# A graph layer and a routed expert layer on one core: two gather pitches in the planner, halved histogram digits, five lists of nodes, and a short write behind each long counting step

## The chip, the cores and the metric

The kernel runs on one core of a Trainium2 chip, as one launch. The metric is the device time of that launch in microseconds (us); the time shown for a kernel is the median of several runs, and one further execution is recorded by the hardware profiler.

The engines that occur below: TensorE (PE in the profile, PEld its weight loads) for matrix products, VectorE (DVE) and ScalarE (ACT) for elementwise work, GpSimd (POOL), which here mostly issues indirect DMAs (gathers and scatters by a list of row numbers), and SyncE (SP), which issues plain DMAs. Each engine runs its own instructions in program order and waits on semaphores for the others.

## The reference

`x` holds 128 graphs of 128 nodes with 256 features, 16384 nodes in all.

```python
# layer 0: graph layer, then a mixture of experts
x = x + gnn(layernorm(x), adj)        # relu((x + adj @ x) W1 + b1) W2 + b2, per graph
x = x + ffn(layernorm(x), edge_index)

# ffn
h = (x @ W_gat).reshape(M, HEADS, NUM_EXPERTS)            # 4 heads x 4 experts
src, dst = edges + self loops                             # 1048576 random edges
e = leaky_relu(a_src[src] + a_dst[dst], 0.2)
ee = exp(e - segment_max(e, dst)[dst])
alpha = ee / segment_sum(ee, dst)[dst]
agg = segment_sum(h[src] * alpha[:, :, None], dst) + b_gat
scores = layernorm(agg).reshape(M, HEADS, NUM_EXPERTS).mean(1)
topk_s, topk_i = top_k(scores, 2)
w = softmax(topk_s)
for ei in range(NUM_EXPERTS):
    g = where(topk_i == ei, w, 0).sum(-1)
    out = out + g * (gelu(x @ W1[ei] + b1[ei]) @ W2[ei] + b2[ei])
```

The numbers in `edge_index` run over 65536, four times the nodes, so about three targets in four lie outside and drop out of the sums. Which two experts a node takes depends on the attention over all of its edges, so an expert can be chosen only once the edges are sorted, gathered and summed.

## The kernel before

**Stage 1** (0 to about 690 us) computes the graph layer graph by graph and writes `x1` and its layernorm to HBM, with a table of 24 numbers a node for the attention (`table`: h, a_src, a_dst). Beside it the edges are prepared for the attention.

**Stage 2** (690 us to the end) has four strands.

*Counting* (`count_edges`, VectorE). Every partition holds 8192 edge targets as int16 numbers. `Runs` sorts them in runs by a network of maximum and minimum steps, most of them 2048 numbers long (`build`, L529, `_pairs`, L502, `merge`, L546, which keeps the larger half), `push` (L653, L659) then moves the sorted targets into cells, and `histogram` (L699) counts them: in 8 sets of 512 cells, VectorE writes a low digit (L720, L724) and a high digit (15 comparisons `is_ge`, L730) as 0 and 1, and TensorE multiplies the two (L738, 64 products of 128x64 a set) into counts, which ScalarE copies out. There is one buffer for the high digits; before it is written again the products of the set before must have read it.

*Gathering* (`Gathers.task`, GpSimd). The attention runs over blocks of 47 columns of edges; each column of the first 12 blocks is one indirect DMA of 128 rows (L866), 564 in all. Only a few blocks' buffers exist, so that block k+3 is begun when block k has been used. `ask` puts other indirect DMAs into the same queue: one "last row", 128 `fin` rows (states of finished nodes), 94 `r_x` gathers (rows of nodes for routed units) and 94 `out_dram` writes (L873). `wait` adds small copies (`seen`, L857).

*Attention* (`attend`, VectorE). Each block takes a dozen steps on VectorE (L1069 to L1130). For a 13th block `last_block` gathers the rows that it lacks as one more DMA (`e<-table,e`), spreads them by L1022 on VectorE and three products on TensorE (L1031). Blocks from the fifth on wait until the counts are there. As soon as enough blocks are done, `finish_attention` and `gates` choose the two experts for a range of graphs (`PARTS`, `PIECES`).

*Experts* (TensorE). The graphs 88 to 127 run all four experts on every node (dense units: 16 products at L1537, gelu on ScalarE at L1541, 32 products at L1556). They need no gate at first and fill TensorE while edges are counted. The nodes of graphs 0 to 87 are put into units of 256 that take the same pair of experts (routed units, 47 of them). `Routes.task` makes the lists of nodes for each stretch of graphs (`REACH`, four stretches ending at 32, 64, 82 and 88; the counts of units in them, `LISTED`, are 11, 16, 9 and 11): prefix sums, then for batches of 8 graphs a product of two 0/1 digits (L1464 makes `low`) into one table, from which node numbers and places come, and a DMA on SP that puts the nodes' weights beside their rows (`xr<-weight`). A routed unit gathers its rows (`r_x<-xr,nodes`), turns them by four transposes on TensorE (L1683) and one copy on ScalarE (L1687), runs 32 products at L1702 and 32 at L1556, is weighted on VectorE (L1725, L1735) and written out by GpSimd.

**What sets the order.** In stage 2 the order of instructions on every engine is fixed at build time by a planner (`Plan`): each strand is a Python generator, which issues its instructions, then yields what it thinks they cost (`yield 0.3 * (HHI - 1)`) or a condition (`plan.was("counts")`). `Plan.run` keeps a clock for each of GpSimd, TensorE and VectorE, and lets the engine that is furthest behind take its next task. A gather is put down at `GATHER_US` = 1.4. So a constant that no instruction uses can still move instructions past each other. The names that the following touches: `GATHER_US`, `PART` (gathers in one go), `PARTS`, `PIECES`, `REACH`, `BATCH`, `LOWS` (buffers of `low`), `Runs` and its loops, `push`, `histogram`, `Gathers.task`.

Of the kernel before, what the change touches and what calls it, by code (L numbers as in the profile page):

```python
# [25 lines left out]
P = 128  # L26
# [3 lines left out]
M = NB * P  # L30
# [6 lines left out]
EC = NE // P  # L37
# [16 lines left out]
CKC = 32  # L54
HSET = 512
HK = 8
HLO = 8
HHI = P // HLO
# [6 lines left out]
SECOND_US = 7.5  # L65
BARE_US = 6.95
TURN_US = 0.8
GATHER_US = 1.4
LAND_US = 4.0
AHEAD_US = 6.0  # L70
SCALAR_US = 4.0
# [5 lines left out]
AHEAD = (3, 4, 8)  # L77
AHEAD_BUFS = 2
HIST_US = 2.0
SLACK_US = 20.0  # L80
PART = 6
YIELD_US = 16.0
XBUFS = 7

PARTS = [
    (15, 0, 2), (24, 0, 3), (32, 0, 4), (43, 0, 5), (53, 2, 6), (64, 3, 7),
    (72, 3, 8), (82, 4, 9), (88, 4, 10), (106, 5, 11), (117, 7, 12), (128, 7, 13),
]  # L90
PARTS = [
# [1 line left out]
    for start, (stop, a, b) in zip([0] + [g for g, _, _ in PARTS], PARTS)  # L93
]
PIECES = [slice(a, b) for a, b in zip(
    (0, 32, 64, 82, 88, 106), (32, 64, 82, 88, 106, 128)
)]
MOST = 32
EARLY = 4


REACH = (32, 64, 82, 88)
NL = REACH[-1]
PAIRS = [(a, b) for a in range(X) for b in range(a + 1, X)]
SLOTS = 2 * P
# [9 lines left out]
BAD = 13  # L115
SPREAD = 10
SHIFT = 4
BATCH = 8
LOWS = 2
LIST_US = 0.05  # L120


# [10 lines left out]
class Pair:  # L133


    def __init__(self, a, b):
        self.cur, self.other = a, b
# [350 lines left out]
class Runs:  # L488

    def __init__(self, nc, a, b, length, n):
        self.nc, self.pair, self.length, self.n = nc, Pair(a, b), length, n

    def _pairs(self, d):

        nc, s = self.nc, self.n // self.length
        v = self.pair.cur[:, 0 : self.n].rearrange("p (k t d) -> p k t d", t=2, d=d * s)
        o = self.pair.other[:, 0 : self.n].rearrange("p (k t d) -> p k t d", t=2, d=d * s)
        for t, op in enumerate((ALU.max, ALU.min)):  # L500
            for cols, cost in self._cuts(self.n // 2, d * s):
                nc.vector.tensor_tensor(  # L502
                    o[:, :, t, cols], v[:, :, 0, cols], v[:, :, 1, cols], op=op
                )
                yield cost
        self.pair.swap()

    def _cuts(self, n, inner):
# [10 lines left out]
    def build(self):  # L519

        nc, n, s = self.nc, self.n, self.n // self.length
        run = 1
        while run < self.length:
            v = self.pair.cur[:, 0:n].rearrange("p (k t l s) -> p k t l s", t=2, l=run, s=s)
            o = self.pair.other[:, 0:n].rearrange("p (k t l s) -> p k t l s", t=2, l=run, s=s)
            a, b = v[:, :, 0, :, :], v[:, :, 1, ::-1, :]
            for t, op in enumerate((ALU.max, ALU.min)):
                for cols, cost in self._cuts(n // 2, s):
                    nc.vector.tensor_tensor(  # L529
                        o[:, :, t, :, cols], a[..., cols], b[..., cols], op=op  # L530
                    )
                    yield cost
            self.pair.swap()
            yield from self._clean(run // 2)
            run *= 2

    def merge(self, keep_all):

        nc, n, s = self.nc, self.n, self.n // self.length
        v = self.pair.cur[:, 0:n].rearrange("p (l t s) -> p l t s", t=2, s=s // 2)  # L540
        a, b = v[:, :, 0, :], v[:, ::-1, 1, :]
        out = self.pair.other
        for at, op in ((0, ALU.max), (n // 2, ALU.min))[0 : 2 if keep_all else 1]:
            half = out[:, at : at + n // 2].rearrange("p (l s) -> p l s", s=s // 2)
            for cols, cost in self._cuts(n // 2, s // 2):
                nc.vector.tensor_tensor(half[:, :, cols], a[:, :, cols], b[:, :, cols], op=op)  # L546
                yield cost
        if keep_all:
            d = self.length // 2
            self.pair.swap()  # L550

            self.length *= 2
            yield from self._clean(d)
        else:
            self.n //= 2
            self.pair.swap()
            yield from self._clean(self.length // 2)
# [13 lines left out]
def count_edges(tc, nc, c, sp, dram):  # L571

    raw = [c.counted_raw] + [sp.tile([P, 4096], I32, name=f"raw{i}") for i in range(2)]
    pick = picks(nc, sp)
    runs = Runs(nc, c.counted, raw[1].bitcast(I16), 32, EC)
    yield from runs.build()
    yield from runs.merge(False)
    yield from runs.to_one()
# [54 lines left out]
    low = dst.bitcast(F32)  # L633
# [17 lines left out]
    def push(value, moved, by, rate):  # L651
        for v in halves(w, 2 if rate == 1 else 1):
            nc.vector.tensor_single_scalar(  # L653
                moved[:, v], value[:, v], P * by, op=ALU.bitwise_xor
            )
            yield w / 1920 / 2 + 0.1
        for v in halves(w - by, 4 // rate):
            to = slice(v.start + by, v.stop + by)
            nc.vector.tensor_tensor(value[:, to], moved[:, v], value[:, to], op=ALU.min)  # L659
            yield (w - by) / 960 / 4 + 0.1  # L660

    by = CROW // 2
    while by >= P:
# [31 lines left out]
def by_group(t):  # L695
    return t.rearrange("p (g k) -> p g k", k=HK)


def histogram(nc, c, value, raw, pick, sp):  # L699


    plan = c.plan


    w = P * CKC
    n_sets, per = w // HSET, HSET // CKC
    low = sp.tile([P, HSET], I16, name="low_digit")
    high = raw[1].bitcast(BF16).rearrange("p (g h k) -> p g h k", h=HHI, k=HK)
    lows = raw[2].bitcast(BF16).rearrange(
        "p (b g l k) -> p b g l k", b=2, l=HLO, k=HK  # L710
    )
    nc.vector.memset(high[:, :, 0], 1.0)
    yield 0.6
    found = raw[0].bitcast(F16)
    cols = per * HLO * HK
    taken = plan.after(0.0)
    for s in range(n_sets - 1, -1, -1):
        cells = slice(s * HSET, (s + 1) * HSET)
        one = lows[:, s % 2]
        nc.vector.tensor_single_scalar(  # L720
            low, value[:, cells], 2 * M - 1 - (P - HLO), op=ALU.bitwise_and
        )
        for j in range(HLO):
            nc.vector.tensor_single_scalar(  # L724
                one[:, :, j], by_group(low), float(j), op=ALU.is_equal
            )
        yield 0.3 * (HLO + 1)
        yield taken
        for j in range(1, HHI):
            nc.vector.tensor_single_scalar(  # L730
                high[:, :, j], by_group(value[:, cells]), float(HLO * j), op=ALU.is_ge
            )
        yield 0.3 * (HHI - 1)
        yield plan.after(0.5)
        pt = c.ps_big.tile([P, G, D], F32, name="big").rearrange("p g d -> p (g d)")
        for b in range(per):
            for g in range(b * CKC // HK, (b + 1) * CKC // HK):
                nc.tensor.matmul(  # L738
                    pt[:, b * HLO * HK : (b + 1) * HLO * HK],
                    high[:, g].rearrange("p h k -> p (h k)"),  # L740
                    one[:, g].rearrange("p l k -> p (l k)"),
                    start=(g % (CKC // HK) == 0), stop=((g + 1) % (CKC // HK) == 0),
                )
        taken = plan.tensor(HIST_US, 1.0)
        nc.scalar.copy(found[:, s * cols : (s + 1) * cols], pt)
    yield taken
# [89 lines left out]
class Gathers:  # L836
# [50 lines left out]
    def block(self, k):  # L887

        pool = self.ahead if k in AHEAD else self.ga
        return pool.tile([P, CB, ROW], F32, name="hs")  # L890

    def ask(self, todo, name, how=None, soon=False):

        at = len(self.asked)
        if soon:
            at = sum(entry[3] for entry in self.asked)
        self.asked.insert(at, (todo, name, how or self.one, soon))

    def task(self):
# [6 lines left out]
        while True:  # L906
            self.wait()
            if self.asked:
# [6 lines left out]
                yield GATHER_US * len(now)  # L915
                if not rest:
                    plan.done(name, LAND_US)
            elif parts and self.room(parts[0][0]):
# [11 lines left out]
                for i in range(j.start, j.stop):  # L930
                    col = k * CB + i
                    self.one(self.rows[k][:, i, :], self.table, self.c.index[:, col : col + 1])
                yield GATHER_US * (j.stop - j.start)
                if j.stop == CB:
                    plan.done(f"block{k}", LAND_US)
            elif not parts and {"routed end", "ends end"} <= plan.at.keys():
# [1741 lines left out]
```

## Time and profile before

| what | us |
|---|---|
| runs | 2082.5, 2083.95, 2087.71 |
| median | 2083.95 |
| profiled execution | 2084.91 |
| its span (first to last instruction) | 2083.1 |
| TensorE busy in it | 1925.0 |
| VectorE busy | 1505.7 |
| GpSimd busy | 1103.7 |
| ScalarE busy | 846.5 |

The granted TensorE clock of that execution is 0.971 of full speed on the mean. The span in stretches, busy time of each engine:

| stretch (us) | PE | DVE | POOL | PEclk |
|---|---|---|---|---|
| 700 to 775 | 75.0 | 71.8 | 64.7 | 1.00 |
| 775 to 800 | 13.7 | 5.4 | 19.7 | 0.80 |
| 800 to 1000 | 200.0 | 196.2 | 164.4 | 1.00 |
| 1000 to 1025 | 25.0 | 2.1 | 19.1 | 1.00 |
| 1025 to 1140 | 95.7 | 89.6 | 93.2 | 0.91 |
| 1140 to 1321 | 181.0 | 76.1 | 141.2 | 1.00 |
| 1321 to 1425 | 102.8 | 81.8 | 81.8 | 1.00 |
| 1425 to 1460 | 24.1 | 3.6 | 20.4 | 0.80 |
| 1460 to 1850 | 369.3 | 239.0 | 293.3 | 1.00 |
| 1850 to 2084 | 207.9 | 157.4 | 100.9 | 0.96 |

How to read the lines that follow. A line of the waits names the engine, what it was about to write and its line, and after the arrow who released it: microseconds in total, how often, the longest. A line of the groups names line, engine, operation, output and input tiles with their shapes and the count; then busy time and the mean nanoseconds of one; then the idle time before them and what ended it. In a timeline, each line is a stretch of equal instructions: start, length, engine, line, and how many. [...]

### The profile page before, as it was taken

What the parts mean: (1) busy time and instruction counts of PE and PEld (TensorE: products, weight loads), DVE (VectorE), ACT (ScalarE), POOL (GpSimd) and SP (SyncE); (2) the same over time, 40 slices, a digit from 0 to 9 for tenths busy, and PEclk for the clock granted to TensorE, in tenths of its full rate; (3) what the DMA queues carried; (4) which work ended last, traced back from release to release, by engine and by line L of the source; (5) the groups of instructions that cost most, each with busy time, mean ns of one, the idle gap of its engine ahead of it and who ended that gap; (6) DMA issues with size and microseconds to landing.
All of it is one profiled execution on the core that took longest, in us unless ns stands there. A gap on an engine that the chain in (4) does not pass through costs nothing. (4 is left out here: it accounts for less than half of the span.)

```text
span 2083.1 us, 28131 instructions
## 1 busy us (share of the span) xinstructions
PE 1925.0 (92%) x8882; PEld 1443.8 (69%) x8882; DVE 1505.7 (72%) x3758; ACT 846.5 (41%) x1533; POOL 1103.7 (53%) x1064
## 2 busy tenths in 40 slices
PE   7999989889998897999969999997999999999996
PEld 4676667666666464666647666786888888788785
DVE  5989999849997887999585571473438768567586
ACT  5878544444453222333313333341333444344332
POOL 2110101110100888888887777776777777766431
PEclk9999989999998899999989999998999999999998
DMA  9988887696852211233131246325554466477865
GB/s 238 226 223 212 196 233 187 177 203 160 135 134 74 57 48 49 60 124 124 31 104 51 56 144 235 104 72 168 157 190 129 142 169 146 119 186 260 289 228 180
DMA packets 299122, 313.36 MB, mean 150 GB/s; under 512 B 111617, under 2 KB 239571, under 8 KB 298838
## 3 DMA queue, kind: packets, MB, share of 16 engines
q1 hardware_dynamic: 231350, 241.19, 36.6%
q0 software_dynamic: 67616, 70.28, 18.5%
q8 instruction: 75, 1.23, 0.2%
q14 instruction: 81, 0.66, 0.1%
HBM read 156.93 MB, written 130.32 MB: 138 GB/s over the span
## 5 line engine op out<-in xcount | busy, mean ns | idle before, releaser
L866 POOL DMA_INDIRECT hs<-table,index x564 | 643.6, 1141 | 166.7 <-issue 159.8
L1556 PE MATMUL big<-mw,m_hid 128*128 (+1 forms) x2784 | 628.3, 383 | 0.0
L1556 PEld LDWEIGHTS big<-mw,m_hid 128*128 128x128 f32 x2784 | 524.9, 191 | 85.8 <-issue 17.0
L1702 PE MATMUL m_phid<-m_xn,mw 128*128 128x256 f32 x1504 | 341.9, 385 | 31.1 <-ACT m_xn L1687 28.9
L1702 PEld LDWEIGHTS m_phid<-m_xn,mw 128*128 128x128 f32 x1504 | 285.6, 192 | 76.5 <-ACT m_xn L1687 34.6
L1563 ACT COPY m_out<-big 128x1024 f32<-128x1024 f32 x87 | 88.1, 1012 | 510.5 <-PE big L1556 504.7
L1537 PE MATMUL m_phid<-m_xn,mw 128*128 128x512 f32 x640 | 286.0, 598 | 10.2 <-issue 10.2
L1955 POOL DMA_DIRECT2D at<-in_adj_dram x31 | 41.9, 1353 | 433.7 <-DMA at<-self_eye 376.3
L2037 PE MATMUL big<-w_sb,hid 128*128 128x256 f32 x1024 | 238.9, 389 | 11.9 <-ACT h_t L2018 11.5
L2026 PE MATMUL p_hid<-h_t,w_sb 128*128 128x512 f32 x512 | 232.1, 603 | 10.5 <-ACT h_t L2018 7.2
L2037 PEld LDWEIGHTS big<-w_sb,hid 128*128 128x128 f32 x1024 | 195.5, 195 | 43.0 <-ACT h_t L2018 17.4
L1537 PEld LDWEIGHTS m_phid<-m_xn,mw 128*128 128x128 f32 x640 | 122.1, 192 | 144.9 <-issue 134.4
L1708 ACT ACTIVATE m_hid<-m_phid,r_b 128x256 f32<-128x256 f32 x376 | 155.7, 472 | 157.0 <-PE m_phid L1702 105.4
L2026 PEld LDWEIGHTS p_hid<-h_t,w_sb 128*128 128x128 f32 x512 | 94.7, 192 | 118.8 <-issue 97.9
L1541 ACT ACTIVATE m_hid<-m_phid,mb 128x512 f32<-128x512 f32 x160 | 109.1, 687 | 146.3 <-PE m_phid L1537 146.2
L866 POOL DMA_INDIRECT fin<-states,ends x128 | 137.8, 1077 | 37.6 <-issue 35.6
L1735 DVE SCALAR_TENSOR_TENSOR r_x<-m_out,r_x 128x256 f32<-128x256 f32 x188 | 87.0, 484 | 71.9 <-ACT m_out L1563 62.0
L866 POOL DMA_INDIRECT r_x<-xr,nodes x94 | 98.1, 1044 | 40.9 <-issue 26.5
L2030 ACT ACTIVATE hid<-p_hid,b_sb 128x512 f32<-128x512 f32 x128 | 87.1, 682 | 76.8 <-PE p_hid L2026 76.7
L873 POOL DMA_INDIRECT out_dram<-r_x,places x94 | 100.4, 1068 | 32.1 <-issue 14.7
L2009 POOL DMA_DIRECT2D xt<-b_sb x32 | 43.1, 1347 | 104.5 <-ACT xn L1893 57.3
L1725 DVE SCALAR_TENSOR_TENSOR r_x<-b_rows,r_x 128x256 f32<-128x256 f32 x188 | 86.8, 483 | 4.5 <-issue 1.1
(393 smaller groups left out, 2444.5 us busy)
## 6 DMA issues: line engine op xcount, KB each, us to landing
mw<-in_L_ffn_W_dram SPq DMA_DIRECT2D x102, 512.0 KB
states<-room SPq DMA_DIRECT2D x55, 564.0 KB
ys<-m_out SPq DMA_DIRECT2D x40, 512.0 KB
y_in<-ys SPq DMA_DIRECT2D x40, 512.0 KB
xt<-in_x_dram SPq DMA_DIRECT2D x32, 512.0 KB
xt<-b_sb POOLq DMA_DIRECT2D x32, 512.0 KB
x_d<-x SPq DMA_DIRECT2D x32, 512.0 KB
xn_d<-xn_t SPq DMA_DIRECT2D x32, 512.0 KB
```

Of the source, the lines that this page charges most:

```text
L866: self.nc.gpsimd.indirect_dma_start(out=out, out_offset=None, in_=rows, in_offset=bass.IndirectOffsetOnAxis(ap=index, axis=0),)
L873: sc = self.nc.gpsimd.indirect_dma_start(out=rows, out_offset=bass.IndirectOffsetOnAxis(ap=index, axis=0), in_=values, in_offset=None, bou ...
L1537: nc.tensor.matmul(p_hid, w1[:, k, f * P : (f + 1) * P], xn[:, k, :], start=(k == 0), stop=(k == 1),)
L1541: nc.scalar.activation(hid[:, f, :], p_hid, AF.Gelu, bias=b1[:, f : f + 1])
L1556: nc.tensor.matmul(p_y[:, s, :], hid[:, f, s * P : (s + 1) * P], w2[s // 2][:, f, :], start=(f == 0 and not b2), stop=(f == DH // P - 1 an ...
L1563: nc.scalar.copy(y, p_y)
L1702: nc.tensor.matmul(p_hid[:, half], w1[i][:, k, f * P : (f + 1) * P], xt[:, k, :], start=(k == 0), stop=(k == 1),)
L1708: nc.scalar.activation(hid[:, f, half], p_hid[:, half], AF.Gelu, bias=b1[i][:, f : f + 1])
L1735: self.nc.vector.scalar_tensor_tensor(x[:, s, D : 2 * D], y[:, 2 * i + s, :], x[:, s, 2 * D + i : 2 * D + i + 1], x[:, s, D : 2 * D], op0= ...
L2026: nc.tensor.matmul(p_hid, w1_sb[:, k, f * P : (f + 1) * P], h_t[:, k, :], start=(k == 0), stop=(k == 1),)
L2030: nc.scalar.activation(hid[:, f, :], p_hid, AF.Relu, bias=b1_sb[:, f : f + 1])
L2037: nc.tensor.matmul(p_y[:, s, :], hid[:, f, s * P : (s + 1) * P], w2_sb[:, f, :], start=(f == 0), stop=(f == DH // P - 1),)
```

## The change

It has five parts.

1. The planner puts a gather down at 1.42 us until the counts are there and at 1.33 afterwards (1.4 throughout before), and hands GpSimd three gathers at a time instead of six.
2. Behind each step of `Runs` and `push` whose planned cost is at least 1.0 us, VectorE writes 64 zeros a partition into a tile that nothing reads (`rest`). The program has 156 of these writes.
3. The high digits' buffer is cut in two halves. A set of 512 cells is compared in two halves of 256, each with its own wait for the products that read that half two halves earlier; the products of a set are issued in two halves.
4. The stretch of graphs 32 to 63 is listed in two parts, ending at 52 and at 64: five lists with 11, 10, 6, 9 and 11 units, 47 as before. `PIECES` and one entry of `PARTS` follow. 
5. Lists are made in batches of 6 graphs with three buffers, instead of 8 with two.

```diff
-GATHER_US = 1.4
+GATHER_US = 1.33
+BESIDE_US = 1.42
...
+REST = 64
+REST_US = 0.11
 SLACK_US = 20.0
-PART = 6
+PART = 3
...
-    (15, 0, 2), (24, 0, 3), (32, 0, 4), (43, 0, 5), (53, 2, 6), (64, 3, 7),
+    (15, 0, 2), (24, 0, 3), (32, 0, 4), (43, 0, 5), (52, 2, 6), (64, 3, 7),
...
-    (0, 32, 64, 82, 88, 106), (32, 64, 82, 88, 106, 128)
+    (0, 32, 52, 64, 82, 88, 106), (32, 52, 64, 82, 88, 106, 128)
...
-REACH = (32, 64, 82, 88)
+REACH = (32, 52, 64, 82, 88)
...
-BATCH = 8
-LOWS = 2
+BATCH = 6
+LOWS = 3
...
+    def rest(self, cost):
+
+        if cost < 1.0:
+            return cost
+        self.nc.vector.memset(self.pad, 0.0)
+        return cost + REST_US
...
                 nc.vector.tensor_tensor(
                     o[:, :, t, cols], v[:, :, 0, cols], v[:, :, 1, cols], op=op
                 )
-                yield cost
+                yield self.rest(cost)
...
+    pad = sp.tile([P, REST], F32, name="pad")
+    runs = Runs(nc, c.counted, raw[1].bitcast(I16), 32, EC, pad)
...
-            yield w / 1920 / 2 + 0.1
+            yield runs.rest(w / 1920 / 2 + 0.1)
...
-            yield (w - by) / 960 / 4 + 0.1
+            yield runs.rest((w - by) / 960 / 4 + 0.1)
...
-    taken = plan.after(0.0)
+    taken = [plan.after(0.0)] * 2
...
-        yield 0.3 * (HLO + 1)
-        yield taken
-        for j in range(1, HHI):
-            nc.vector.tensor_single_scalar(
-                high[:, :, j], by_group(value[:, cells]), float(HLO * j), op=ALU.is_ge
-            )
-        yield 0.3 * (HHI - 1)
-        yield plan.after(0.5)
+        yield 0.2 * (HLO + 1)
         pt = c.ps_big.tile([P, G, D], F32, name="big").rearrange("p g d -> p (g d)")
...
+        for half in range(2):
+            high = highs[:, half]
+            begin = s * HSET + half * HSET // 2
+            yield taken[-2]
+            for j in range(1, HHI):
+                nc.vector.tensor_single_scalar(
+                    high[:, :, j], by_group(value[:, begin : begin + HSET // 2]),
+                    float(HLO * j), op=ALU.is_ge,
+                )
+            yield 0.15 * (HHI - 1)
+            yield plan.after(0.5)
+            for b in range(half * per // 2, (half + 1) * per // 2):
+                for g in range(b * CKC // HK, (b + 1) * CKC // HK):
+                    nc.tensor.matmul(
...
+            taken.append(plan.tensor(HIST_US / 2, 1.0))
...
+    def pitch(self):
+        return GATHER_US if "counts" in self.plan.at else BESIDE_US
...
-                yield GATHER_US * (j.stop - j.start)
+                yield self.pitch() * (j.stop - j.start)
```

More of the change, by code (lines that the diff above doesn't have):

```diff
@@ L488, with __init__ @@
 class Runs:
-    def __init__(self, nc, a, b, length, n):
+    def __init__(self, nc, a, b, length, n, pad):
         self.nc, self.pair, self.length, self.n = nc, Pair(a, b), length, n
+        self.pad = pad
+    def rest(self, cost):
[3 more added lines that the diff above has]
+        return cost + REST_US
     def _pairs(self, d):
@@ L531, in build @@
                     )
-                    yield cost
+                    yield self.rest(cost)
             self.pair.swap()
@@ L546, in merge @@
                 nc.vector.tensor_tensor(half[:, :, cols], a[:, :, cols], b[:, :, cols], op=op)
-                yield cost
+                yield self.rest(cost)
         if keep_all:
@@ L574, in count_edges @@
     pick = picks(nc, sp)
-    runs = Runs(nc, c.counted, raw[1].bitcast(I16), 32, EC)
+    pad = sp.tile([P, REST], F32, name="pad")
+    runs = Runs(nc, c.counted, raw[1].bitcast(I16), 32, EC, pad)
     yield from runs.build()
@@ L707, in histogram @@
     low = sp.tile([P, HSET], I16, name="low_digit")
-    high = raw[1].bitcast(BF16).rearrange("p (g h k) -> p g h k", h=HHI, k=HK)
+    highs = raw[1].bitcast(BF16).rearrange(
+        "p (b g h k) -> p b g h k", b=2, h=HHI, k=HK
+    )
     lows = raw[2].bitcast(BF16).rearrange(
@@ L711, in histogram @@
     )
-    nc.vector.memset(high[:, :, 0], 1.0)
+    nc.vector.memset(highs[:, :, :, 0], 1.0)
     yield 0.6
@@ L715, in histogram @@
     cols = per * HLO * HK
-    taken = plan.after(0.0)
+    taken = [plan.after(0.0)] * 2
     for s in range(n_sets - 1, -1, -1):
-        cells = slice(s * HSET, (s + 1) * HSET)
         one = lows[:, s % 2]
         nc.vector.tensor_single_scalar(
-            low, value[:, cells], 2 * M - 1 - (P - HLO), op=ALU.bitwise_and
+            low, value[:, s * HSET : (s + 1) * HSET], 2 * M - 1 - (P - HLO),
+            op=ALU.bitwise_and,
         )
@@ L726, in histogram @@
             )
-        yield 0.3 * (HLO + 1)
-        yield taken
-        for j in range(1, HHI):
-            nc.vector.tensor_single_scalar(
-                high[:, :, j], by_group(value[:, cells]), float(HLO * j), op=ALU.is_ge
-            )
-        yield 0.3 * (HHI - 1)
-        yield plan.after(0.5)
-        pt = c.ps_big.tile([P, G, D], F32, name="big").rearrange("p g d -> p (g d)")
[L736 to L742, printed above, removed]
-                )
-        taken = plan.tensor(HIST_US, 1.0)
+        yield 0.2 * (HLO + 1)
+        pt = c.ps_big.tile([P, G, D], F32, name="big").rearrange("p g d -> p (g d)")
+        for half in range(2):
[6 more added lines that the diff above has]
+                    float(HLO * j), op=ALU.is_ge,
+                )
+            yield 0.15 * (HHI - 1)
[3 more added lines that the diff above has]
+                    nc.tensor.matmul(
+                        pt[:, b * HLO * HK : (b + 1) * HLO * HK],
+                        high[:, g % (HSET // 2 // HK)].rearrange("p h k -> p (h k)"),
+                        one[:, g].rearrange("p l k -> p (l k)"),
+                        start=(g % (CKC // HK) == 0), stop=((g + 1) % (CKC // HK) == 0),
+                    )
+            taken.append(plan.tensor(HIST_US / 2, 1.0))
         nc.scalar.copy(found[:, s * cols : (s + 1) * cols], pt)
-    yield taken
+    yield taken[-1]
     yield plan.after(2.0)
@@ L914, in task @@
                     self.asked.insert(0, (rest, name, how, soon))
-                yield GATHER_US * len(now)
+                yield self.pitch() * len(now)
                 if not rest:
```

## The prediction

> **What bounds the kernel now.** I read the busy shares first, then TensorE's waits behind stage 1, then those of VectorE and GpSimd, and last the timelines in which gathers meet counting.
>
> ```profile
> PE 1925.0 (92%) x8882; PEld 1443.8 (69%) x8882; DVE 1505.7 (72%) x3758; ACT 846.5 (41%) x1533; POOL 1103.7 (53%) x1064
> PE m_phid L1702 <- ACT m_xn L1687: 28.9, 24, 1.3
> PE big L738 <- DVE counted L730: 19.3, 1, 19.3
> PE pt L1031 <- DVE room L1022: 11.3, 1, 11.3
> PE m_phid L1537 <- issue: 10.2, 1, 10.2
> PE big L1683 <- DMA r_x<-xr,nodes: 10.0, 4, 4.7
> ```
>
> TensorE sets the time, and what can still be had is in these lines (total, times, longest, from 650 us on): one stall of 11.3 before the copied last row's products, one of 19.3 before the first histogram, 24 turns of 1.2, and 10.0 for rows of routed units. (The 10.2 of L1537 is before 690 and untouched.) The two long stalls go back to VectorE, and from there to gathers:
>
> ```profile
> DVE e L1083 <- DMA hs<-table,index: 23.1, 2, 22.8
> DVE room L1022 <- DMA e<-table,e: 21.8, 1, 21.8
> ```
>
> VectorE waits 21.8 for the one-row gather (GpSimd reaches it at 791.6), and 22.8 from 1000 to 1023 for block 3's last gather, the 204th, begun at 1020.4. So GpSimd's pace beside counting is behind both. Two timelines of 843 to 851 us (start, length) show that pace, first GpSimd, then VectorE:
>
> ```profile
> 845.52 0.95 POOL L866 DMA_INDIRECT hs<-table,index  x1 [0.30 <-issue]
> 846.78 1.96 POOL L866 DMA_INDIRECT hs<-table,index  x1 [0.30 <-issue]
> 849.05 0.95 POOL L866 DMA_INDIRECT hs<-table,index  x1 [0.30 <-issue]
> ```
> ```profile
> 845.56 2.36 DVE L502 TENSOR_TENSOR counted<-raw 128x2048 int16<-128x2048 int16 x2
> 847.96 2.36 DVE L502 TENSOR_TENSOR raw<-counted 128x2048 int16<-128x2048 int16 x2
> ```
>
> A gather that begins just ahead of a step takes 0.95 and the next follows 1.26 later; one that meets a running step takes 1.96, pitch 2.27. The extreme: seven gathers record as back to back for 7.86 us at 722 and the stretch moves at 2.5 each.
>
> **The change, part by part.** By the program order of before and after:
>
> *Rests.* 156 writes of 64 numbers join VectorE. The nearest rows:
>
> ```profile
> L1066 DVE MEMSET msg<- 128x20 f32 x1 | 0.1, 75 | 0.0
> L1050 DVE MEMSET pre<- 128x384 f32 x2 | 0.8, 378 | 0.1
> ```
>
> By interpolation 75 + 44/364 x 303 = 112 ns. A counting step is 1.14 start to start without a semaphore wait and 1.26 with one, mean 1.20; I take step plus rest as 1.25, which is +0.05 x 156 = 8 us. Ends: -6 if the rest lies wholly inside the wait that it displaces, +30 if each adds 0.11 and a second gap of 0.08. These 8 lie ahead of L1083 and the histogram, where VectorE has 22.8 of wait to pay with.
>
> What they buy is the gathers' pace. No row shows a gather beside such a write, so bounds: 1.26 if one always slips in, 2.27 if never. Between 700 and 1020 the pitch now is (1020.4 - 722.3)/181 = 1.65. I take 1.4: a stop each 1.25 us, nearly the gather's own 1.26, nearest the rows of 843 to 845. Then 181 x (1.65 - 1.4) = 45 us earlier at most; a later start and blocks' buffers eat part, so I put gather 204 at 984 instead of 1020, and the one-row gather at 773.
>
> [...]
>
> *The 11.3 at L1031.* With the row gathered 18 earlier and L1022 done by 779, TensorE, which arrives at 786, waits for nothing: -11.3, and -1.2 of slow clock behind it.
>
> *The 19.3 at L738.* VectorE reaches L1083 at about 980 (999 less the 21.8 it waited at L1022, plus rests), waits some 7 (0 to 22), and has the first half set ready at 1051 to 1062. The order puts one more dense unit (14.5) ahead of the histogram, so TensorE, which was there at 1057.5 (1076.81 less 19.34), comes at 1057.5 - 12.5 + 14.5 = 1059.5. Stall 0 to 3: -19 from the stall, and -1.6 since the first 64 products took 3.60 on a slowed clock against 2.03 later.
>
> *Halved digits.* 120 comparisons become 240. From 1073.41 on, 15 of them take 3.35, 0.223 each; the smallest operations of VectorE follow each other at 0.075 (the copies at 999.03, 999.10 and 999.17), so half the elements cost about 0.075 + 0.148/2 = 0.15: 240 x 0.15 - 120 x 0.223 = +9 us (ends 0 and +27). Per set VectorE then needs 9 x 0.23 + 30 x 0.15 = 6.6, beside TensorE's 7 us of expert products between two sets: hidden if just. 512 products stay 512.
>
> *Five lists.* Nodes of graphs 32 to 63 are listed in two goes. The order gains 52 list products (0.03 each), 52 operations of `low`, a further gates piece, four table loads of ScalarE (1.28 each, ScalarE is 41% busy): about +4 us with the half-set switches on TensorE, of which a wait for the second list's total, 0 to 2. VectorE's part lies beside routed units, where it is 239 of 390 us busy. The two pitches, the parts of three gathers and the batches of six issue nothing: they act through the order, which is counted here. In exchange, turns that stand directly ahead of their unit fall from 24 to 17: -7 x 1.2 = -8.5. There is also one more transfer of weights on SP's queue, for which GpSimd waits, with block gathers and later units' rows queued behind it:
>
> ```profile
> POOL r_x L866 <- DMA xr<-weight: 8.9, 1, 8.9
> ```
>
> Up to there the first routed unit's turn moves from 1321.8 to about 1292 (-11 -1 -19 -2 +4, rounded). TensorE alone would end its last product at 2007: before 2060, less 30, less 8.5, less about 16 us lost at units 7 and 8 (10.0 waiting, the rest clock).
>
> *GpSimd takes it back.* From block 3 on it works through a list of DMAs in fixed order:
>
> ```profile
> L866 POOL DMA_INDIRECT hs<-table,index x311 | 321.1, 1032 | 93.0 <-issue 87.3 <-DMA hs<-table,index 2.1 <-DMA r_x<-xr,nodes 0.9
> L866 POOL DMA_INDIRECT r_x<-xr,nodes x70 | 71.6, 1024 | 30.7 <-issue 19.4 <-DMA xr<-weight 8.9 <-PE m_phid L1702 1.5
> L866 POOL DMA_INDIRECT fin<-states,ends x74 | 71.6, 968 | 21.7 <-issue 20.4 <-DMA fin<-states,ends 0.6 <-ACT m_hid L1541 0.3
> L873 POOL DMA_INDIRECT out_dram<-r_x,places x60 | 62.5, 1042 | 19.1 <-issue 10.2 <-DVE r_x L1735 2.2 <-DVE low L1464 1.2
> ```
>
> In 1140 to 1850 that is 515 DMAs; less 10 of waits, 700/515 = 1.36 each. In the new order unit 31's rows are the 789th DMA from the first gather (now the 762nd). So they start at 984 + 585 x 1.36 + 9 for weights = 1789 and land 3.7 later, at 1793, while TensorE alone would be there at 1769: up to 24 us of new waits at L1683 between units 7 and 31. From unit 31 the order is TensorE's again: 238 to the last product (before 246, less its turns), and 23 from there to the end of the span. 1793 + 238 + 23 = 2054 for the span. The profiled execution was 1.8 over its span and 1.0 over the median, so the median comes at about 2054.5; I say 2054.
>
> **Rivals.** *Rests pay in full* (2041 to 2065): the above, gather 204 between 971 and 995.
>
> *No gather passes in a rest* (slower). The seven gathers that record as one block at 722, beside gaps of 0.04, speak for it; the quick passes ahead of a step speak against. GpSimd then stays at 1020, but the order asks unit 31's rows 27 DMAs later: 1020 + 585 x 1.36 + 9 + 4 = 1829, 15 behind today's 1814; with 238 + 23 and a few us of slow clock in those waits the time is 2095 (2090 to 2110). The dense unit drawn ahead fills a stall with work that is then missing later. It decides once gather 204 starts later than about 1013.
>
> *Half of it* (2065 to 2088): pitch near 1.5, gather 204 at 996 to 1012, or each of five weight transfers holding GpSimd 9 us at a bad moment.
>
> *GpSimd never binds* (2028 to 2041): its pitch falls to 1.30, as it is between 1075 and 1100 where few waits fall. 975 + 585 x 1.30 + 4 = 1740, ahead of TensorE's 1769, and 2007 + 23 = 2030 is left.
>
> **How the numbers follow.** Chances: full 0.52, half 0.22, none 0.16, never bound 0.10. The time is the first's; its own range is 2041 to 2065. The range 2036 to 2088 leaves out none passing and most of the last. A measurement tells 0.3% (6.3 us) from nothing: faster is below 2077.7, slower above 2090.2. Faster: 0.52 + 0.10 + 0.14 of the half case = 0.76; slower 0.16; same 0.08.
>
> **What would show it.** Right: gathers at 1.35 to 1.45 between 720 and 980; the waits at L1031 and L738 under 3; VectorE's wait at L1083 under 20; the first routed turn at 1285 to 1298; about 17 waits for m_xn; new waits of TensorE for `r_x`, 10 to 25 us in all. Wrong: gather 204 behind 1010 (rests don't pass); VectorE's counting steps over 1.30 with their rest (price); a histogram wait above 6 with gathers early (halved digits too dear); waits for `r_x` at nought, or above 40.

## The result, and the profile after

The changed kernel takes 2092.0 us in the median of 8 runs (2091.26 to 2097.43), the kernel before 2081.26 in 8 (2076.24 to 2087.71): ratio 1.0053, 95% interval 1.0035 to 1.0070. It is slower, by half a per cent. The forecast was 2054 and faster; the rival in which no gather passes in a rest said 2095. The profiled execution has a span of 2092.6 (2083.1 before).

Several chips took part, and on some of them TensorE's short products started 0.7 to 2.8 us apart from the histogram on and every kernel, the one before too, took 2310 to 2360, so that of those runs (e1 to e4, e13 to e16) only what lies ahead of the histogram is compared with the rest.

The busy shares and TensorE's waits from 650 us on, in the changed kernel (L1704 is L1683 of before, L1723 is L1702, L756 is L738, L1052 is L1031):

```profile
PE 1924.5 (92%) x8938; PEld 1442.9 (69%) x8938; DVE 1555.9 (74%) x4262; ACT 851.4 (41%) x1539; POOL 1107.6 (53%) x1064
```
```profile
PE big L1704 <- DMA r_x<-xr,nodes: 29.4, 6, 18.7
PE m_phid L1723 <- ACT m_xn L1708: 22.1, 16, 2.8
PE big L756 <- DVE counted L748: 12.2, 1, 12.2
PE m_phid L1558 <- issue: 10.1, 1, 10.1
PE m_phid L1723 <- DMA mw<-in_L_ffn_W_dram: 6.5, 1, 6.5
...
PE pt L1052 <- DVE room L1043: 2.6, 1, 2.6
```

TensorE is busy for the same 1925 us, so the loss is waits. Those ahead fell, if not all as far as meant: 11.3 to 2.6 at the last row, 19.3 to 12.2 at the histogram, 28.9 to 22.1 at the turns. The wait for rows of routed units rose from 10.0 to 29.4, and the one for expert weights from 2.0 to 6.5. VectorE's waits between 690 and 1140 are nearly what they were (23.1 and 21.8):

```profile
DVE e L1104 <- DMA hs<-table,index: 21.0, 1, 21.0
DVE room L1043 <- DMA e<-table,e: 20.4, 1, 20.4
```

So the gathers came hardly sooner. The timelines of GpSimd and of VectorE (start, length) show why; L503 is the new write:

```profile
721.72 1.99 POOL L884 DMA_INDIRECT hs<-table,index  x1 [0.30 <-issue]
724.01 2.00 POOL L884 DMA_INDIRECT hs<-table,index  x1 [0.30 <-issue]
726.32 2.00 POOL L884 DMA_INDIRECT hs<-table,index  x1 [0.30 <-issue]
728.63 0.95 POOL L884 DMA_INDIRECT hs<-table,index  x1 [0.31 <-issue]
```
```profile
721.70 0.11 DVE L503 MEMSET pad<- 128x64 f32 x1
721.73 1.16 DVE L513 TENSOR_TENSOR raw<-counted 128x2048 int16<-128x2048 int16 x1
...
724.00 0.11 DVE L503 MEMSET pad<- 128x64 f32 x1
724.03 1.16 DVE L540 TENSOR_TENSOR counted<-raw 128x2048 int16<-128x2048 int16 x1
...
728.61 0.11 DVE L503 MEMSET pad<- 128x64 f32 x1
728.68 1.23 DVE L513 TENSOR_TENSOR raw<-counted 128x2048 int16<-128x2048 int16 x1
```

At 721.70 and 724.00 the next step starts 0.03 us after the write does, the write still running by its record. Each of the first three gathers starts 0.01 to 0.02 after a write's start and is held for a whole step. It then ends so that its successor comes 2.29 to 2.31 later, which is two steps of 1.15: at the same point of the step, to be held again. At 728.61 the next step has a semaphore to wait for and starts 0.07 after the write, and the gather that comes between them passes. Of the gathers 23 to 204, these start between two operations of `Runs` of over 1 us each, by how long ahead of the next one:

| ahead of the step | before: passed, held | changed: passed, held |
|---|---|---|
| 0 to 25 ns | 3, 0 | 0, 19 |
| 26 to 100 ns | 31, 0 | 17, 0 |
| 101 to 500 ns | 2, 2 | 14, 0 |
| over 500 ns | 0, 27 | 0, 19 |

In the kernel before, a gather that comes in the last 100 ns ahead of the next step gets in, 34 of 34 (and in e1 and e11 below, without the write, all 9 that come in the last 25). With the write, it depends on what comes behind it. In the changed kernel the 19 gathers that start between a write and a long step of `Runs` 0.03 behind it are all held, the 15 ahead of a step that a semaphore keeps back to 0.07 all pass, and so do the 14 that start in the 0.15 us ahead of a write with no such semaphore behind it. Over the eight traces with writes of 64 (this one, e5, e9, e10, e13, e14, e16, e17) the three counts are 149 of 152 held, 128 of 128 passed and 108 of 108 passed. So in these traces a gather had to be there before the write started, as it had to be there before the step; beside the write it got in only where a semaphore kept the step back. Over all 181, 119 pass (records up to 1.2 us) and 61 are held (1.2 to 2.4; before 116 and 63); the pitch is 1.607 (1.647), and gather 204 starts at 1012.6 (1020.4; forecast 984).

One thing the writes do change. In the kernel before, a single gather is held through six steps that follow each other:

```profile
722.33 7.86 POOL L866 DMA_INDIRECT hs<-table,index  x1 [0.30 <-issue]
```
```profile
721.30 3.52 DVE L502 TENSOR_TENSOR raw<-counted 128x2048 int16<-128x2048 int16 x3
724.71 4.66 DVE L529 TENSOR_TENSOR counted<-raw 128x2048 int16<-128x2048 int16 x4
```

Each of the eight traces without writes (before, e1, e6, e7, e8, e11, e15, e18) has one such record of 7.9 to 9.0 us between 712 and 723; the eight with writes of 64 have none over 3.3. It is worth little: from the queue's first DMA to the 204th it is 327.5 us in the changed kernel, 332.9 and 332.7 in e1 and e11.

What follows is one order of DMAs on GpSimd. Unit 31's rows are the 789th, as forecast, and start at 1813.6, which is (1813.6 - 1012.6)/585 = 1.369 each. The dearest wait is at unit 7, here on TensorE and on GpSimd:

```profile
1430.02 0.44 PE L1704 MATMUL big<-ident,r_x 128*128 128x128 f32 x1 [18.66 <-DMA r_x<-xr,nodes]
```
```profile
1423.49 0.96 POOL L884 DMA_INDIRECT r_x<-xr,nodes  x1 [0.30 <-issue]
1424.75 0.96 POOL L884 DMA_INDIRECT r_x<-xr,nodes  x1 [0.30 <-issue]
```

From 1300 to these two no wait of GpSimd is over 0.3: it is simply not there yet. TensorE, whose first turn comes 10.4 earlier than before, gets to unit 7 ahead of rows that start only 2.9 earlier.

### The profile page after: what moved, and what is told of

The parts are those of the page before. It is cut to its first block, busy times and chain, and to the rows that moved or that the text cites. A ratio compares the mean times of both kernels' runs of the same rounds, so it can differ in the third digit from the quotient of the medians.

```text
span 2092.6 us, 28770 instructions
## 1 busy us (share of the span) xinstructions
PE 1924.5 (92%) x8938; PEld 1442.9 (69%) x8938; DVE 1555.9 (74%) x4262; ACT 851.4 (41%) x1539; POOL 1107.6 (53%) x1064
## 5 line engine op out<-in xcount | busy, mean ns | idle before, releaser
L884 POOL DMA_INDIRECT hs<-table,index x564 | 631.9, 1120 | 165.1 <-issue 155.8
L1723 PE MATMUL m_phid<-m_xn,mw 128*128 128x256 f32 x1504 | 340.9, 383 | 31.4 <-ACT m_xn L1708 22.1
L1723 PEld LDWEIGHTS m_phid<-m_xn,mw 128*128 128x128 f32 x1504 | 283.8, 191 | 73.1 <-ACT m_xn L1708 25.9
L1558 PE MATMUL m_phid<-m_xn,mw 128*128 128x512 f32 x640 | 287.6, 600 | 13.5 <-issue 10.1
L891 POOL DMA_INDIRECT out_dram<-r_x,places x94 | 106.0, 1127 | 31.5 <-issue 14.7
L884 POOL DMA_INDIRECT r_x<-xr,nodes x94 | 104.6, 1113 | 33.1 <-issue 25.1
```

Source lines behind the costliest of these rows:

```text
L884: self.nc.gpsimd.indirect_dma_start(out=out, out_offset=None, in_=rows, in_offset=bass.IndirectOffsetOnAxis(ap=index, axis=0),)
L891: sc = self.nc.gpsimd.indirect_dma_start(out=rows, out_offset=bass.IndirectOffsetOnAxis(ap=index, axis=0), in_=values, in_offset=None, bou ...
L1558: nc.tensor.matmul(p_hid, w1[:, k, f * P : (f + 1) * P], xn[:, k, :], start=(k == 0), stop=(k == 1),)
L1723: nc.tensor.matmul(p_hid[:, half], w1[i][:, k, f * P : (f + 1) * P], xt[:, k, :], start=(k == 0), stop=(k == 1),)
```

## The experiments: the writes

**e1, e11: the changed kernel's order without the writes.**

```diff
-        self.nc.vector.memset(self.pad, 0.0)
+        pass
```

> The changed kernel in its own order, without the 156 writes. Theory (the writes of 64 numbers, seen 0.03 us before the next step, are too short to let a gather in, and cost as little): gathers 23 to 204 keep a pitch of 1.60 to 1.66, gather 204 at 1010 to 1020, the time 2090 to 2098, ratio to before 1.004 to 1.009. Rival (the writes as built do let some in, and save the kernel from worse): pitch 1.75 or more, gather 204 behind 1030, 2103 to 2115.

> The kernel of e1 once more, with no writes in the changed kernel's order. Theory (the writes of 64 numbers move nothing): gather 204 at 1008 to 1020, ratio 1.002 to 1.008. Rival (they let gathers in): gather 204 behind 1025, ratio 1.010 or more.

Gather 204 at 1010.5 and 1016.9, pitch 1.586 and 1.585: without the writes the gathers from the 23rd on are no slower (1.607 with them; the long hold comes ahead of the 23rd in e1 and e11). e11's time is 2094.92, ratio 1.0041 (1.0025 to 1.0057), against 1.0053 with the writes: the intervals overlap. e1's time can't be compared. The writes are not what made the kernel slower, and gain nothing that the time shows. They cost next to nothing either: mean step 1.192 with and 1.178 without.

**e2, e3, e4, e12: writes of 128, 192 and 256 numbers, same order.**

```diff
-REST = 64
+REST = 256
```

> The changed kernel with writes of 128 numbers. Theory: a write of 128 is seen some 0.08 us before the next step, so step and write are 1.23; a gather that was held starts 0.13 ahead of a step and passes, and about one in four is held: pitch 1.45 to 1.55, gather 204 at 985 to 1000, the histogram's stall under 6, the time 2065 to 2082. Rival (a write of any length lets nothing in): pitch 1.60 or more, VectorE 8 us later per 156 writes, the time 2092 to 2102.

> The changed kernel with writes of 192 numbers. Theory: step and write are 1.28 or more, longer than a free gather's 1.26, so that nearly every gather passes: pitch 1.28 to 1.40, gather 204 at 965 to 985, stalls before the histogram and at the routed units 7 and 28 under 5 each, the time 2045 to 2070. Rival (a write of any length lets nothing in): pitch 1.60 or more, the histogram 10 to 20 us later than in the changed kernel, the time 2095 to 2115.

> The changed kernel with writes of 256 numbers. Theory: pitch 1.27 to 1.38 as with 192, but VectorE pays 0.19 to 0.2 for each write, some 8 us more in all than with 192, all ahead of the histogram: it is ready 0 to 8 later, the time 2045 to 2075, no better than with 192. Rival (a write of any length lets nothing in): pitch 1.60 or more, the time 2105 to 2125.

> The kernel of e4 once more, writes of 256 numbers in the changed kernel's order, where the chip before held TensorE back behind the histogram. Theory (writes this long let the gathers in, and those that are still held meet other operations): gather 204 at 992 to 1003, some 10 to 20 us ahead of the changed kernel, the histogram's stall under 9, waits for r_x of 10 to 20 us instead of 29, ratio 0.996 to 1.002. Rival (what GpSimd gains VectorE loses): ratio 1.004 or more.

The step is the mean from one step of `Runs` of 2048 numbers to the next where nothing but the write stands between them (99 pairs from 690 on).

| run | numbers | step | passed, held | pitch | gather 204 |
|---|---|---|---|---|---|
| e11 | none | 1.178 | 123, 57 | 1.585 | 1016.9 |
| changed | 64 | 1.192 | 119, 61 | 1.607 | 1012.6 |
| e2 | 128 | 1.236 | 133, 47 | 1.565 | 1005.9 |
| e3 | 192 | 1.290 | 143, 36 | 1.607 | 1014.5 |
| e4 | 256 | 1.357 | 143, 36 | 1.529 | 997.9 |
| e12 | 256 | 1.356 | 143, 35 | 1.569 | 1010.9 |

The same kernel's gather 204 differs by 6 to 13 us from chip to chip (e1 and e11; e4 and e12; 1009.3, 1016.1 and 1010.8 in e13, e16 and e17), so differences of that size in the last column say nothing.

Half of the theory stands: with longer writes more gathers get in. Of those between long steps of `Runs`, 66 pass at 101 to 300 ns ahead in e3, and 76 at 301 to 500 in e4; they start before the write does. In e2 the step follows 0.08 behind the write's start without a semaphore, and 4 of the 5 that start in between are held, so that it is hardly the distance that counts. But the pitches that I expected, 1.45 to 1.55 in e2 and 1.27 to 1.40 in e3 and e4, are missed, the latter by far, for three reasons that the traces show. Gathers that pass at each step go at the step's pace (the seven from 857.79 on in e4 start 1.34 to 1.36 apart), and the mean step is now 1.357 there. Of the 36 that are still held in e3 and in e4, 14 start between two long steps even so, and the rest meet other operations, of `attend` and of the counting. And in e3 GpSimd waits 19.6 us in seven `seen` copies, for marks that ScalarE sets. In e12 three gathers in a row are held for 10.5, 5.1 and 6.5 us from 716 on, in e4 none for over 2.9: most of what parts these two runs of one kernel lies there. e12's ratio is 1.0016 (0.9986 to 1.0047), so with 256 numbers the time can't be told from the kernel before, nor surely from the changed one.

## The experiments: the parts one at a time

**e6: the accounts and parts of three alone**, in the kernel before.

```diff
-GATHER_US = 1.4
+GATHER_US = 1.33
+BESIDE_US = 1.42
-PART = 6
+PART = 3
```

> The kernel before with the two pitches and parts of three alone. The order asks unit 31's rows as the 789th DMA, as the changed kernel does, instead of the 762nd. Theory (accounts): the stalls of 11 and 19 us stay, turns that stand directly ahead fall by five or six (7 us), and new waits for r_x of 15 to 35 us come, ratio 1.003 to 1.012. Rival (other parts of the change lose): ratio 0.994 to 1.001.

2099.95 beside 2081.55, ratio 1.0104 (1.0054 to 1.0153). TensorE's waits in it:

```profile
PE m_phid L1706 <- ACT m_xn L1691: 19.9, 17, 1.3
PE big L739 <- DVE counted L731: 18.2, 1, 18.2
PE big L1687 <- DMA r_x<-xr,nodes: 18.1, 9, 6.3
PE m_phid L1706 <- DMA mw<-in_L_ffn_W_dram: 12.4, 3, 6.6
```

Seven turns fewer stand ahead of their unit (9 us), the waits for rows grow by 8 and those for expert weights by 10, and 6.3 for a digit of the lists comes new: this part alone is slower, by constants that no instruction uses. Why the weights came late is not shown. Parts of three were not tried without the accounts; e10 and e17 below have them and are not slower than the kernel before.

**e7: the five lists alone. e8: the halved digits alone.** The diffs are parts 4 and 5, and part 3, of the change.

> The kernel before with five lists, pieces and batches of six alone; unit 31 stays the 762nd. Theory (accounts): nothing much, ratio 0.996 to 1.003. Rival (the fifth list costs): one more wait of GpSimd for weights of 9 us or a wait of TensorE for the second list's product, ratio 1.004 to 1.010.

> The kernel before with halved digits alone. Theory: 240 comparisons at 0.15 cost VectorE 9 us more than 120 at 0.223, spread over the sets and hidden beside TensorE but for the first, whose products begin after half of it, 1 us earlier: ratio 0.997 to 1.002. Rival (VectorE falls behind TensorE in the eight sets): waits at the histogram's products of 1 us and more in several sets, 5 to 15 us in all, ratio 1.003 to 1.008.

e7: 2084.75, ratio 1.0020 (1.0007 to 1.0033); e8: 2080.44, 0.9999 (0.9985 to 1.0014). Neither makes the loss; e7's 0.2% is the more of the two. In e8 TensorE waits 20.2 before the first set and not measurably in the others: the extra work of VectorE is hidden.

**e5, e9, e10: other accounts in the changed kernel**, the rest as it is.

```diff
-GATHER_US = 1.33
-BESIDE_US = 1.42
+GATHER_US = 1.37
+BESIDE_US = 1.6
```

(e9: 1.37 and 1.55; e10: 1.4 for both.)

> The changed kernel with the two pitches put down as its profile measures them: 1.6 beside counting, 1.37 afterwards. The order then asks the rows of routed unit 7 as the 451st DMA from the first gather instead of the 500th, those of unit 31 as the 723rd instead of the 789th. Theory (the accounts of 1.42 and 1.33 are below what GpSimd does, and the order made from them has TensorE wait for rows): waits for r_x fall from 29.4 us to under 8, and the time to 2058 to 2074, ratio to before 0.989 to 0.997. Rival (the loss comes from the five lists, the halved digits or the writes, whatever the accounts): the time stays at 2086 to 2098.

> The changed kernel with pitches of 1.55 beside counting and 1.37 afterwards. The order lies between the changed kernel's and e5's: unit 31's rows are the 759th DMA (789 and 723 there, 762 before), the last row of finished nodes the 843rd (835 and 871 there, 847 before). Theory (one GpSimd queue feeds two ends, TensorE's last unit and the sums of the dense units, and the accounts share it out): waits for r_x under 12 us, TensorE's last product at 2040 to 2058, the last sum within 15 us of it, the time 2060 to 2078, ratio 0.990 to 0.998. Rival (the rest of the change costs, too): 2079 or more.

> The changed kernel with the old single pitch of 1.4: unit 31's rows are the 750th DMA, the last row of finished nodes the 849th, 20 turns directly ahead of their unit. Theory (two ends): TensorE's last product at 2040 to 2058, the last sum at 2055 to 2070, the time 2064 to 2082, ratio 0.991 to 1.000. Rival (the rest of the change costs, too): 2083 or more.

e5, with the pitches that the profile itself shows, is as slow as e6: 2098.01, ratio 1.0084 (1.0066 to 1.0103). The waits for rows did fall, to 6.3, and TensorE ends at 2035.5, 40 us sooner than in the changed kernel. But the kernel doesn't end there. The last chain of waits of e5:

```profile
2068.81 8.60 DMA y_in<-ys
2077.46 0.04 issue
2077.50 0.50 DVE acc L2283
...
2086.28 2.19 DVE acc L2283 x6
```

The dense units' outputs are weighted and summed on VectorE (`acc`) when the gates of the graphs 88 to 127 are known, and these need the `fin` rows, which GpSimd fetches from the same queue. In e5 the last `fin` gather is the 871st and starts at 1991.6; in the changed kernel it is the 835th, at 1916.5. I hadn't seen this second end. e9's order turned out otherwise than its expectation says (unit 31's rows the 729th, the last `fin` the 861st): 2088.25, ratio 1.0008 (0.9995 to 1.0020). e10: 2086.77, ratio 1.0013 (0.9998 to 1.0027).

**e13 to e18: 1.36 and 1.35 behind the counts.**

```diff
-GATHER_US = 1.33
+GATHER_US = 1.36
```

> The changed kernel with pitches of 1.42 beside counting, as it has, and 1.36 afterwards instead of 1.33. Its order has 17 turns directly ahead, like the changed kernel's, unit 31's rows as the 759th DMA (789 there) and the last row of finished nodes as the 843rd (835 there). Theory (one GpSimd queue feeds two ends and what one gains the other loses; over seven runs on undisturbed chips TensorE's last product and the last sum add up to 4112 to 4133): both ends come at 2048 to 2066, sum 4105 to 4125, the time 2066 to 2082, ratio 0.992 to 0.999. Rival (the parts other than the accounts cost as much as they gain): ratio 1.001 or more.

> The changed kernel with 1.42 and 1.35: unit 31's rows as the 774th DMA, the last row of finished nodes as the 839th, 16 turns directly ahead. Theory (two ends): between the changed kernel and e13, TensorE's last product at 2056 to 2070, the last sum at 2040 to 2056, ratio 0.995 to 1.002. Rival (waits for r_x jump once the order is ahead of GpSimd at all): ratio 1.003 or more.

> The kernel of e13 in its own order without the 156 writes. Theory (writes of 64 numbers do nothing): within 0.3% of e13, gather 204 within 8 us of it. Rival (they are what makes e13 what it is): 0.4% or more slower than e13, gather 204 10 us later or more.

> The kernel of e13 once more (pitches of 1.42 and 1.36; unit 31's rows the 759th DMA, the last row of finished nodes the 843rd), since e13's chip issued TensorE's short products 0.7 to 2.6 us apart, the kernel before's too. Theory (two ends of one GpSimd queue): TensorE's last product and the last sum both at 2048 to 2066, the time 2066 to 2084, ratio 0.992 to 1.000. Rival (the parts other than the accounts cost as much as they gain): ratio 1.001 or more.

> The kernel of e13 a third time, in search of a chip on which the kernel before takes its 2081 to 2085. Theory (two ends of one GpSimd queue): TensorE's last product and the last sum both at 2048 to 2066, the time 2066 to 2084, ratio 0.992 to 1.000. Rival (the parts other than the accounts cost as much as they gain): ratio 1.001 or more. On a chip where the kernel before takes 2320 or more it tells nothing of either.

> The kernel of e17 without the 156 writes. Theory (writes of 64 numbers do nothing): ratio 0.989 to 0.996, gather 204 within 8 us of e17. Rival (they have a part in it): ratio 0.997 or more. On a chip where the kernel before takes 2320 or more it tells nothing of either.

e13 to e16 ran where TensorE's instructions came late (ratios 1.0020, 1.0018, 1.0067 and 1.0075, beside 2324 and 2330 for the kernel before) and settle nothing on the question; so e14's pitch of 1.35 stays open. e17, the same kernel as e13, has 2065.27 beside 2079.39: ratio 0.9925 (0.9901 to 0.9949). It is faster than both kernels. e18, without the writes, has 0.9919 (0.9900 to 0.9938): they have no part in it. The gain holds only where the kernel before takes about 2081: on the other chips this same kernel has 1.0020 (e13) and 1.0075 (e16). TensorE's waits in e17:

```profile
PE m_phid L1723 <- ACT m_xn L1708: 20.4, 17, 1.5
PE big L756 <- DVE counted L748: 13.1, 1, 13.1
PE big L1704 <- DMA r_x<-xr,nodes: 11.4, 4, 9.4
```

All but the last are nearly as in the changed kernel. The two ends side by side, from the traces (us; "routed" is from the first routed turn to TensorE's last product):

| kernel | unit 31's rows, last `fin` (DMA number) | first turn | TensorE's last product | routed | last sum |
|---|---|---|---|---|---|
| before | 762, 847 | 1321.8 | 2066.1 | 744.3 | 2067.2 |
| changed | 789, 835 | 1311.4 | 2075.5 | 764.1 | 2039.4 |
| e6 | 789, 837 | 1312.6 | 2079.7 | 767.1 | 2047.4 |
| e17 | 759, 843 | 1306.6 | 2048.9 | 742.3 | 2038.1 |
| e10 | 750, 849 | 1317.2 | 2058.9 | 741.7 | 2069.9 |
| e9 | 729, 861 | 1305.5 | 2041.4 | 735.9 | 2082.0 |
| e5 | 723, 871 | 1286.5 | 2035.5 | 749.0 | 2089.5 |

Rows of routed units late: TensorE's end is late. Rows late in favour of them: the last sum is. Against my theory the two do not simply add up: 4105 to 4125 was expected in e17 and its sum is 4087; the last sum, expected at 2048 to 2066, came at 2038.1. One reading of that, which no run tests, lies in GpSimd's longest pauses: in the changed kernel it stands 19.0 us before 1853.9 and 21.6 before 1969.0 in a `seen` copy, until ScalarE has set a mark; in e17 no pause between two of its DMAs from 1200 to 1990 is over 13.5. The first of the two lies ahead of the last `fin` gather (1916.5) and can have delayed the last sum; the second lies behind it and cannot. So where TensorE falls behind the order for want of rows, GpSimd may later be held by what TensorE hasn't done yet.

## Why the prediction was wrong

**The step that failed** is the gathers' pace under the writes: "I take 1.4: a stop each 1.25 us", and from it gather 204 at 984. Measured are a pitch of 1.607 and 1012.6, 28.6 us later: most of the 38.6 by which the span of 2054 was missed. Two things in it were wrong. The write's price: 0.112 us by its record, as interpolated, but only 0.03 of it before the next step starts, so that step and write are 1.15 to 1.22, not 1.25. And the idea that a write is a stop: a gather that starts beside one is held unless a semaphore keeps the next step back, and e1 and e11 show that the pitch is no slower without it. The ends that I gave, 1.26 and 2.27, held the measured one; what I chose between them was not the nearest row but a hope for a new one. The nearest was the pitch measured over the same stretch, 1.65. A reading was wrong, too: the record of 7.86 us at 722 is not seven gathers but one (x1), held through six steps, and so no evidence for the rival that no gather passes.

**A second step failed behind it**, the path to the end: "1793 + 238 + 23" lets unit 31's rows set the time. Their second gather starts at 1813.6, but TensorE turns them at 1827.3, 13.7 later and without a wait, where 3.7 to land was reckoned (1427.63 to 1431.33, the second of unit 7 in the kernel before). GpSimd's rows held TensorE earlier, at units 7 (18.7) and 28 (9.8), 29.4 in all where 10 to 25 was said.

**What rested on it.** The wait at L1104 was to shrink to some 7 and stayed at 21.0, so VectorE had the first half set ready at 1077 instead of 1051 to 1062, and TensorE, there at 1065 (forecast 1059.5), waited 12.2 and not 0 to 3. The first turn came at 1311.4, 19 later than the forecast 1292.

**What held.** The stall at the last row fell by 8.7, 5.0 of it since the rows came sooner (the row gather starts at 785.5, forecast 773, before 791.6) and 3.7 since TensorE comes half a dense pass later. Halved digits: 240 comparisons at 0.153 (0.15 said) for 120 at 0.222, 10 us on VectorE (9 said), hidden: in the rows of 1040 to 1150 VectorE is idle for 2.6 us ahead of the 240 operations, where it waited 24.5 ahead of the 120, and TensorE waits for them only ahead of the first set.

```profile
L748 DVE TENSOR_SCALAR counted<-raw 128x256 bf16<-128x256 int16 x240 | 38.1, 256 | 2.6 <-PE big L756 2.4
L503 DVE MEMSET pad<- 128x64 f32 x21 | 2.4, 112 | 0.0
```

The 156 writes, put at 8 us, cost about 2: 156 x 0.014, by the mean step of e11 and of the changed kernel (1.178 and 1.192). Most of a write's record of 0.112 lies under the next step, which starts 0.03 behind the write's start. Nor does a write let a gather in by itself: of the 19 that start between a write and a step 0.03 behind it, none passed.

Turns: 17 said, 16 seen. GpSimd from block 3 on: 585 DMAs at 1.36 and 9 for weights, 805 in all; measured 801. With 1012.6 put in for 984, the forecast's own sum gives 1012.6 + 805 + 3.7 + 238 + 23 = 2082 for the span, and the rival's, with some us of slow clock, 2095; the span was 2092.6. That the rival's number came so near is partly luck: it had gather 204 at 1020 and unit 31's rows landed at 1829, 7 and 12 us too late, and left out that TensorE would be behind these rows. The point that I gave for where the change turns into a loss, gather 204 behind 1013, is within a microsecond of where it came, but decides nothing: e18 has it at 1018.5 and is faster than the kernel before. What the rival had wrong is its order of causes: not the writes lose, the accounts do (e6, e17), since they ask for rows at a pace that GpSimd hasn't got: 1.33 behind the counts where 1.369 was measured, and with 1.36 the wait for rows fell from 29.4 to 11.4.

**What I had not looked at** is the second end. I followed TensorE to its last product and took the rest of the span as a tail of 23 us. (By the records that product ends at 2066.1 and not at 2060, and the tail is 17; the sum is the same.) In the kernel before the last sum came at 2067.2, one microsecond after TensorE's last product; that both ends fall together there was in its trace, and a DMA moved forward for one may then be paid by the other.

**Open.** Why single gathers are held through several steps, for 7.9 to 9.0 us once in each trace without writes and for 10.5, 5.1 and 6.5 in e12, where the others get in at the next. Why the changed kernel loses less than e6 does, if it does: e6's four runs spread from 2092 to 2113. What makes TensorE's instructions late on some chips was not tried.

## What to carry to other kernels

A planner's cost constant is part of the schedule: 0.03 us a DMA in one of them moved TensorE's last product by 27 us (changed kernel and e17). When two chains are fed from one queue, look at both ends before moving one. The account that makes the order best need not be the true pitch: of the pairs tried here 1.36 with 1.42 won, and 1.37 with 1.6, as measured, lost. An idle instruction was no pause here (149 of 152 gathers beside one were held where no semaphore kept the next step back): before counting on one, measure what gets in, by the phase at which the other engine's instructions start and whether they are held.

## What the runs showed of the hardware that was not expected

In the changed kernel a held gather's turnaround of 2.30 us against a step of 1.15 locks the two engines into a rhythm in which each gather is held: three in a row at 721.72, 724.01 and 726.32. The lock breaks at 728.63, where a semaphore wait puts the next step 0.07 behind the write instead of 0.03 and the gather passes in 0.95. Over eight traces 149 of 152 gathers that started between a write and a step 0.03 behind it were held, and none of 128 where a semaphore kept the step back to 0.07. A gather is mostly held for one step (of the changed kernel's gathers 23 to 203, 61 of the 62 held ones last 1.2 to 2.4 us), but not always: records of 7.9 to 9.0 us, one in each trace without writes, run through six or seven. A write of 64 numbers delays what follows it by about 0.01 us, one of 256 by 0.18 (mean steps 1.178, 1.192, 1.357).
